# Two layers of cross-attention and quantised feed-forward: merged clips and exponentials, one moved rounding, a division in two parts, halved last products

## The chip, the cores and the metric

The kernel runs on one core of one Trainium2 chip. The metric is the device time of one execution in microseconds (us). The core has five engines that work beside each other: TensorE (PE: matmuls, and transposes as matmuls; PEld are its weight loads), VectorE (DVE), ScalarE (ACT), GpSimd (POOL) and SyncE (SP, which here only issues DMAs). Data lie in SBUF, in 128 partitions; matmuls write to PSUM, which is used in banks of 128 x 512 float32.

## What is computed

The input x has 8 batches of 112 tokens with 512 features, the context has 8 batches of 375 rows. Four residual steps follow each other:

```
x = x + L0_xattn(layernorm(x), ctx, mask0)   # one head, softmax over masked context rows
x = x + L0_ffn(layernorm(x), w1, w2, w3)     # silu(gate) * up, then down; each a "bit linear"
x = x + L1_xattn(layernorm(x), ctx, mask1, Wq, Wk, Wv, Wo, ...)   # 16 heads of 32
x = x + L1_ffn(layernorm(x), wq_gate, wq_up, wq_down, scales)     # integer weights - 128, scaled
```

A bit linear rounds its activations to whole numbers of -128..127 by the row's largest value and its weights to -1, 0, 1, and multiplies those. The steps that the change touches:

```
# L0_ffn:   h = silu(bitlinear(xn, w1)) * bitlinear(xn, w2);  x + bitlinear(h, w3)
# L1_xattn: scores = clip(q k^T / sqrt(32), -50, 50), masked ones -50
            probs = softmax(scores);  ctx = probs v;  out = layernorm(0.05-scaled ctx Wo + bo)
# L1_ffn:   y = silu(h Wg * sg) * (h Wu * su);  x + (y Wd) * sd
```

## The kernel before, in words

The 896 tokens (8 x 112) are kept as 7 tiles of 128 rows (`tokens`, `xs[i]`), the hidden size 1408 as 11 blocks of 128. PE's and SP's instructions stand in program order as written; for long stretches DVE, ACT and POOL do so too (`tc.manual_schedule`), elsewhere the framework orders these three when the program is built. A tile of a pool is handed out again only when the instructions that use it are done, so pools add waits of their own.

The keys and values of the second attention (L194 and L203, evicted by L197 and L205) don't depend on anything else. They are produced by a generator, and `fill(n)` puts n of its steps where PE would wait otherwise.

**First feed-forward (L533 to L700).** For each tile i, `gate_up0` multiplies the turned, rounded row (bf16) with ternary weights in three column blocks: four gate matmuls into one PSUM tile, four up matmuls into another (L541), SiLU on ACT (L545), the product on DVE (L546). `ranges0` finds the quantiser's factor `fwd` (L293 to L303, small DVE steps). `round0` (L565) rounds the 1408 columns: one ACT step that adds a large constant (L567), and two POOL steps that take it off again (L570); it also forms a small factor on DVE (L308). `turn_gate0(i + 1)` (L355) transposes the next tile's row on PE (L350) and copies it from PSUM on ACT (L352). `turn_down0` does the same for the rounded 1408 columns, and `down0` multiplies them (L581) and adds the result to the tokens (L583). The loop at L621 calls for each i: `gate_up0(i)`, `ranges0(i)`, filler, `turn_down0(i - 1)`, `round0(i)`, filler, `turn_gate0(i + 1)`, `down0(i - 1)`.

**Queries (L727).** Two groups of tiles (4 and 3), four column blocks each: PE forms a sum of products (L735, L737) and a small correction `less` (L741) in a tile of the pool `ps_s`; DVE takes it off (L745).

**Second attention (L848 to L1000).** Loops over 8 batches b and 3 chunks c of 125 context rows. `scores(b, c)` takes four tiles of one PSUM bank each from `ps_s` (four buffers), one for each r of the four 32-row groups; each holds four heads (dc = 0..3) of 112 tokens, 448 columns. For each r follow a clip on DVE (L907) and an exponential on ACT (L908) into SBUF tiles `sets[...][r]`. `add(b)` sums two chunks' exponentials on POOL (L894; on DVE for the last batch), so that the denominators take two matmuls and not three for each r. `sums` forms denominators (L923) and numerators (L928) in PSUM; ACT copies both (L934, L935). In step c = 1 of the next batch `divide` takes the reciprocal of 4 x 112 columns in one DVE instruction (L939) and multiplies (L941). In step c = 2, `project_product(b - 2)` multiplies tile b - 2 with Wo (L800): the tile's 128 tokens end inside batch b - 1, since 112 isn't 128. `project_begin` and `project_end` add bias, normalise and add to the tokens (L806 to L825; a reciprocal root on POOL, L105 to L109; POOL then forms a factor at L812, which DVE uses at L819). `write4` (L834) and `transpose4` (L841) normalise and turn tile b - 3 for the second feed-forward. In the meantime its integer weights are loaded in pieces of 640 columns and converted (L866, L877, L879). STEPS says in which steps a filler step of keys and values is put; batch 4 has two instead of three.

**Second feed-forward (L1021 to L1068).** `gate_up1` works on a group of tiles (512 or 384 tokens wide). For each hidden block hc it takes a PSUM tile for gate and one for up, again from `ps_s`; eight matmuls into each (L1031, float32r, high and low part), SiLU on ACT (L1036), product on DVE (L1037), a rounded copy on ACT (L1039), the remainder on DVE (L1040). The last tile's output of the attention (`project(NT - 1)`) is put between blocks 1 and 2. Then `down1` multiplies for each of the tiles: 22 matmuls of 512 columns into one PSUM tile (L1049), and `finish` scales it (L1017), adds the tokens (L1018) and stores 128 x 512 values (L1019). Group 1's tiles are turned (L841) between group 0's down products. At run time a branch chooses another form of this stage for large weights (`feed_forward1_wide`), which isn't taken here.

Of the kernel before, what the change touches and what calls it, by code (L numbers as in the profile page):

```python
# [64 lines left out]

SPLIT = 2.0 ** -12
LESS = 1.0 - 2.0 ** -13


@with_exitstack  # L70
def two_layers(ctx: ExitStack, tc: tile.TileContext, x, ctxT, ctxN, mask0, mask1, w1, w2, w3,
# [167 lines left out]
    with tc.tile_pool(name="w0", bufs=1, side="right") as w0p, \  # L239
# [290 lines left out]
        with tc.tile_pool(name="work1", bufs=2, side="right") as work1:  # L530
# [90 lines left out]
            for i in range(2, NT):  # L621
                gate_up0(i)
                if i == 2:
                    steps_of(2, 2)
                elif i == 3:
                    next(preparing[2])
                elif i == 4:
                    next(preparing[3])
                if i == 4:
                    ranges0(i, 1)  # L630
                    next(preparing[3])
                    ranges0(i, 1)
                else:
                    ranges0(i, 2)
                if i == 4:
                    moments2(0)
                    moments2(2)
                elif i == 5:
                    small.append(stat)
                    ve = stat.tile([P, GROUPS[0][1]], F32, name="ln2a_ve")  # L640
                    nc.vector.tensor_scalar_add(ve, mv2[:, :, 1], LN_EPS)
                    rstd2 = rsqrt(ve, "ln2a")
                    small.pop()

                    def normal2(h, i):
                        nc.vector.tensor_scalar(h, xs[i], mv2[:, i, 0:1], rstd2[:, i:i + 1],
                                                ALU.subtract, ALU.mult)
                elif i == NT - 1:
                    for k in range(2):
                        write2(k, normal2, k, work1)  # L650
                fill(2 if i < 4 else 1)
                turn_down0(i - 1)
                if i == 2:
                    steps_of(2, 1)
                round0(i)
                if i == 2:
                    next(preparing[2])
                elif i == 3:
                    next(preparing[3])
                fill(1)  # L660
                if i < NT - 1:
                    turn_gate0(i + 1)
                if i == 2:
                    down0(0)
                    next(preparing[2])
                    next(preparing[2])
                down0(i - 1)
                if i == 3:
# [96 lines left out]
    with tc.tile_pool(name="g1p", bufs=1, side="right") as g1p:  # L765
        h2T[1] = [g1p.tile([P, KC, 384], F32R, name=f"h2T1_{k}") for k in range(3)]
        write = normaliser(xs[4:6], "ln2b")
        for i in range(4, 6):
            write2(i, write, i - 4, tailp)
            transpose2(i, ps_s)()  # L770
        next(asking)
        write2(6, normaliser(xs[6:], "ln2c"), 0, tailp)
        transpose2(6, ps_s)()
        for g in range(2):
            for _ in asking:
                pass
            asking = queries(1)
# [70 lines left out]
    with tc.tile_pool(name="work2", bufs=1, side="right") as work2, \  # L848
# [21 lines left out]
        def convert_integers():  # L870
            for raw, which, half, c, n in loaded:
# [12 lines left out]

        sets = [[work2.tile([P, KC, T], F32, name=f"e{i}{r}") for r in range(NR)]
                for i in range(NCK)]

        def add(b):  # L890
            add = (nc.gpsimd if b in ADD_POOL else nc.vector).tensor_add
            for r in range(NR):
                e, e1 = (sets[(b + c) % NCK][r][:CK] for c in range(2))
                add(e, e, e1)  # L894

        def scores(b, c):
            kT = kvs_of[b][0]
            ss = [ps_s.tile([CK, KC, T], F32, name="s") for r in range(NR)]
            for dc in range(KC):
                for r in range(NR):  # L900
                    rows = slice(r * HD, (r + 1) * HD)
                    nc.tensor.matmul(ss[r][:, dc, :], lhsT=kT[rows, dc, c * CK:(c + 1) * CK],  # L902
                                     rhs=qT[rows, dc, b * T:(b + 1) * T], start=True, stop=True)
            es = sets[(b + c) % NCK]
            for r in range(NR):
                e = es[r][:CK]
                nc.vector.tensor_scalar(e, ss[r], upper[:, c, b:b + 1], -CLIP, ALU.min, ALU.max)  # L907
                nc.scalar.activation(e, e, AF.Exp, scale=SC1)  # L908
            return es

# [25 lines left out]
                rdens[b] = rden  # L936

        def divide(b):
            nc.vector.reciprocal(rdens[b], rdens[b])  # L939
            cols = slice(b * T, (b + 1) * T)  # L940
            nc.vector.tensor_mul(qT[:, :, cols], qT[:, :, cols], rdens[b])  # L941


        STEPS = [3, 3, 3, 3, 2, 3, 3, 3]
# [5 lines left out]
        for b in range(B):  # L950
            for c in range(NCK):
# [18 lines left out]
                if c == 0:  # L970
                    while later:
                        later.pop()()
                    if b >= 3:
                        project_end(b - 3)
                elif c == 1 and b >= 1:
                    divide(b - 1)
                elif c == 2:
                    turned = 3 <= b < 3 + GROUPS[0][1]
                    if turned:
                        write4(b - 3)  # L980
                    if b >= 2:
                        project_product(b - 2)
                    if b == B - 1:

                        hits = ps_s.tile([1, 29], F32, name="s")
# [18 lines left out]
    with tc.tile_pool(name="work3", bufs=2, side="right") as work3, \  # L1004
# [10 lines left out]
        def finish(i, ps):  # L1015
# [2 lines left out]
            nc.vector.tensor_add(y, y, xs[i])  # L1018
            nc.sync.dma_start(out=rows_out[i * P:(i + 1) * P], in_=y)  # L1019

        def gate_up1(g, begin, end, gus):  # L1021

            n = (GROUPS[g][1] - GROUPS[g][0]) * P
# [17 lines left out]
                                     gus[0][:, hc, :n].bitcast(F32))  # L1041

        def down1(g, i, gus):
            ps = ps_d.tile([P, D], F32, name="down")
            j = i - GROUPS[g][0]
            for hc in range(HC):
                w, c = half_of(2, hc * D)
                for k in range(2):
                    nc.tensor.matmul(ps, lhsT=gus[k][:, hc, j * P:(j + 1) * P],  # L1049
                                     rhs=w[:, c:c + D], start=(hc == 0 and k == 0),  # L1050
                                     stop=(hc == HC - 1 and k == 1))
            finish(i, ps)

        def feed_forward1():
            gus = [work3.tile([P, HC, 512], F32R, name=f"gu_{k}", bufs=1) for k in range(2)]
# [3 lines left out]
            for i in range(*GROUPS[0]):  # L1059
# [1 line left out]
                    write4(GROUPS[1][0] + i)  # L1061
                down1(0, i, gus)
                if GROUPS[1][0] + i < NT:
                    transpose4(GROUPS[1][0] + i, ps_s, "s")()
# [5 lines left out]
        def feed_forward1_wide(g):  # L1070
# [27 lines left out]
            for i in range(i0, i1):  # L1098
# [5 lines left out]
                                     start=(hc == 0), stop=(hc == HC - 1))  # L1104
                finish(i, ps)

        is_wide = nc.values_load(wide[0:1, 0:1], min_val=0, max_val=P)
        with tc.If(is_wide == 0) as fits:
            feed_forward1()
        with fits.Else():  # L1110
            project(NT - 1)
            feed_forward1_wide(0)
            for i in range(*GROUPS[1]):
                write4(i)
                transpose4(i, ps_s, "s")()
            feed_forward1_wide(1)


def _laid_out(inputs):
# [63 lines left out]
```

## Time and profile before

| | |
|---|---|
| three runs | 517.44, 517.8, 518.0 us; median 517.8 |
| the profiled execution | 517.36 us, of which the span of instructions is 515.6 |
| granted TensorE clock, mean | 0.996 of full speed |
| DVE, clips L907 | 96 of 125 x 448, mean 676 ns |
| ACT, exponentials L908 | 96 of 125 x 448, mean 570 ns |
| POOL, sums L894 | 28, mean 1233 ns |
| DVE, reciprocals L939 | 8 of 128 x 448, mean 2942 ns |
| PE, last products L1049 | 154 of 128 x 512, mean 396 ns; 22 of them for each tile |
| output DMA | 7 of 256 KB, 2.0 us from issue to landing (median) |

A row of a group gives line, engine, operation, `out<-in` with shapes, and how often; then the busy time in us and the mean of one in ns. A row of the timeline gives the start in us, the duration of a group of like instructions in us, engine, line, names, shapes and count, and in brackets how long the engine had been idle before it and what ended that. Matmuls are pipelined: the end of a record is modelled and several records overlap, so the time that one costs is the step from start to start. A row of the waits gives the total in us, how often, and the longest.

### The profile page before, as it was taken

The numbers are of one execution on the slowest core, as the hardware profiler recorded it, in microseconds if no ns is written. First come the engines' busy times: TensorE is split into PE (matmuls) and PEld (weight loads), VectorE is DVE, ScalarE is ACT, GpSimd is POOL, SyncE is SP. The second block draws the span as 40 slices with busy tenths as digits, with TensorE's granted clock in tenths as the row PEclk, the third lists the DMA queues.
The fourth block names the chain that finished last, engine by engine and source line by source line (L and its number), as shares of the span: only waits on it lengthen the run. The fifth ranks groups of instructions, "written<-read, shape, count | busy, mean of one in ns | idle before, by whom it ended". The sixth has DMA issues, their size and how long they took to land.

```text
span 515.6 us, 8804 instructions
## 1 busy us (share of the span) xinstructions
PE 502.3 (97%) x3380; PEld 315.0 (61%) x3380; DVE 334.3 (65%) x801; ACT 252.4 (49%) x438; POOL 133.9 (26%) x221
## 2 busy tenths in 40 slices
PE   9999999999999999999999999999999999999995
PEld 6445554455545455686565465555555788889983
DVE  3642548767798986964676588997897753334432
ACT  0326656857565665336675375465665233103310
POOL 0000121110011164211551475574753430000000
PEclk9999999999999999999999999999999999999998
DMA  8997795200120100122421112012320000010001
GB/s 242 363 407 298 274 326 201 79 18 0 61 82 1 60 2 0 37 109 58 162 70 53 61 52 62 3 53 62 98 76 5 21 1 1 20 42 20 1 20 46
DMA packets 13343, 45.75 MB, mean 89 GB/s; under 512 B 2081, under 2 KB 3120, under 8 KB 12144
## 3 DMA queue, kind: packets, MB, share of 16 engines
q1 hardware_dynamic: 11744, 41.43, 23.4%
q0 software_dynamic: 1248, 3.70, 2.2%
q8 instruction: 28, 0.46, 0.4%
q14 instruction: 19, 0.16, 0.1%
q10 hardware_dynamic: 304, 0.01, 0.0%
HBM read 41.46 MB, written 1.84 MB: 84 GB/s over the span
## 4 chain that ended last, share of the span: by engine, by line
PE 47%; DVE 6%; POOL 2%; DMA 1%; ACT 1%; issue 1%; DVEq 0%; POOLq 0%
PE s L1031 14%; PE mm L203 8%; PE down L1049 7%; PE mm L800 4%; PE s L902 3%; PE num L928 2%; PE mm L194 2%; DVE e L907 2%; PE den L923 2%; DMA raw<-in_wd_dram 1%; PE mm L737 1%; PE mm L735 1%; PE s L741 1%; DVE e L939 1%; POOL ln_t L108 1%
## 5 line engine op out<-in xcount | busy, mean ns | idle before, releaser
L194 PE MATMUL mm<-cT,wk 128*128 128x375 f32 x256 | 87.6, 487 | 0.0
L203 PE MATMUL mm<-wv,cT 128*125 128x512 f32 x192 | 87.6, 599 | 0.0
L1031 PE MATMUL s<-h4T,w 128*128 128x512 f32 (+1 forms) x352 | 72.6, 367 | 0.2 <-PE num L928 0.2
L1031 PEld LDWEIGHTS s<-h4T,w 128*128 128x128 f32 x352 | 63.5, 188 | 8.8 <-PE num L928 0.5
L907 DVE TENSOR_SCALAR e<-s,upper 125x448 f32<-125x448 f32 x96 | 59.0, 676 | 14.7 <-PE s L902 13.9
L908 ACT ACTIVATE e<-e 125x448 f32<-125x448 f32 x96 | 51.7, 570 | 27.6 <-DVE e L907 27.0
L194 PEld LDWEIGHTS mm<-cT,wk 128*128 128x128 f32 x256 | 47.0, 191 | 27.6 <-issue 0.8
L203 PEld LDWEIGHTS mm<-wv,cT 128*125 128x125 f32 x192 | 34.5, 187 | 38.0 <-issue 36.4
L894 POOL TENSOR_TENSOR e<-e,e 125x448 f32<-125x448 f32 x28 | 33.7, 1233 | 14.9 <-PE num L928 14.9
L1049 PE MATMUL down<-w,gu 128*128 128x512 f32 x154 | 37.0, 396 | 0.0
L541 PE MATMUL mm<-w_q,q_qT 128*128 128x512 fp8e4 (+1 forms) x168 | 34.6, 361 | 1.5 <-ACT q_qT L352 1.1
L439 POOL DMA_DIRECT2D tokens<-x x14 | 10.7, 768 | 90.6 <-DVE x L433 64.0
L1049 PEld LDWEIGHTS down<-w,gu 128*128 128x128 f32 x154 | 28.6, 188 | 6.7
L1039 ACT CAST gu<-gu 128x512 fp32r<-128x512 f32 (+1 forms) x22 | 12.5, 567 | 39.6 <-DVE gu L1037 39.6
L877 ACT ACTIVATE w<-raw,zero_point 128x640 fp32r<-128x640 int32 (+2 forms) x29 | 22.6, 781 | 18.9 <-DMA raw<-in_wd_dram 7.6
L570 POOL TENSOR_SCALAR q<-gu 128x704 bf16<-128x704 f32 x14 | 10.8, 787 | 80.0 <-ACT gu L567 80.0
L902 PE MATMUL s<-qT,kv 32*125 32x112 f32 x768 | 29.3, 280 | 0.6 <-DVE qT L745 0.3
L1037 DVE SCALAR_TENSOR_TENSOR gu<-s,su,gu 128x512 f32<-128x512 f32 (+1 forms) x22 | 15.0, 684 | 21.9 <-PE s L1031 20.6
L902 PEld LDWEIGHTS s<-qT,kv 32*125 32x125 f32 x768 | 24.5, 183 | 7.1 <-issue 5.6
L541 PEld LDWEIGHTS <-q_qT 128*128 128x128 bf16 x168 | 16.4, 98 | 20.3 <-issue 1.8
L879 POOL TENSOR_SCALAR w<-raw 128x640 fp32r<-128x640 int32 (+2 forms) x29 | 19.8, 693 | 34.2 <-ACT w L877 33.9
L800 PE MATMUL mm<-wo,qT 128*128 128x512 f32 x56 | 25.8, 603 | 1.0 <-DVE qT L941 1.0
(236 smaller groups left out, 787.5 us busy)
## 6 DMA issues: line engine op xcount, KB each, us to landing
cT<-in_ctxT_dram SPq DMA_DIRECT2D x13, 750.0 KB, 6.1
raw<-in_w_dram SPq DMA_DIRECT2D x6, 1408.0 KB, 19.2
cN<-in_ctxN_dram SPq DMA_DIRECT2D x8, 768.0 KB, 4.4
raw<-in_wg_dram SPq DMA_DIRECT2D x8, 320.0 KB, 3.1
raw<-in_wu_dram SPq DMA_DIRECT2D x8, 320.0 KB, 3.0
raw<-in_wd_dram SPq DMA_DIRECT2D x8, 320.0 KB, 3.1
out_dram<-d SPq DMA_DIRECT2D x7, 256.0 KB, 2.0
wk<-in_wk_dram SPq DMA_DIRECT2D x4, 256.0 KB, 4.8
```

The costliest lines, as they stand in the source:

```text
L194: nc.tensor.matmul(ps[dc], lhsT=wk_s[:, kc, dc * P:(dc + 1) * P], rhs=cT[:, kc, :], start=(kc == 0), stop=(kc == KC - 1))
L203: nc.tensor.matmul(ps, lhsT=cT[:, kc, c * CK:(c + 1) * CK], rhs=wv_s[:, kc, :], start=(kc == 0), stop=(kc == KC - 1))
L541: nc.tensor.matmul(ps[:, :n], lhsT=qT[:, kc, :], rhs=w[:, kc * H + n0:kc * H + n0 + n], start=(kc == 0), stop=(kc == KC - 1))
L800: nc.tensor.matmul(ps, lhsT=qT[:, kc, i * P:(i + 1) * P], rhs=wo_s[:, kc, :], start=(kc == 0), stop=(kc == KC - 1))
L877: nc.scalar.activation(t, raw, AF.Square, bias=zero_point, accum_out=squares[:, k:k + 1])
L879: nc.gpsimd.tensor_scalar(t, raw, -128.0, 1.0, ALU.add, ALU.mult)
L894: add(e, e, e1)
L902: nc.tensor.matmul(ss[r][:, dc, :], lhsT=kT[rows, dc, c * CK:(c + 1) * CK], rhs=qT[rows, dc, b * T:(b + 1) * T], start=True, stop=True)
L907: nc.vector.tensor_scalar(e, ss[r], upper[:, c, b:b + 1], -CLIP, ALU.min, ALU.max)
L908: nc.scalar.activation(e, e, AF.Exp, scale=SC1)
L1031: nc.tensor.matmul(ps[:, :n], lhsT=w[:, c:c + P], rhs=h4T[k][:, kc, :n], start=(kc == 0 and k == 0), stop=(kc == KC - 1 and k == 1))
L1049: nc.tensor.matmul(ps, lhsT=gus[k][:, hc, j * P:(j + 1) * P], rhs=w[:, c:c + D], start=(hc == 0 and k == 0), stop=(hc == HC - 1 and k == 1))
```

## The change

Five edits:

1. The pool `ps_s` (four tiles of one bank) becomes a pool of two tiles of two banks. `scores` takes two of these pairs and puts r = 0, 1 into the first and r = 2, 3 into the second. Clips, exponentials and POOL's sums handle a pair (2 x 448 columns) in one instruction. All else that took tiles from `ps_s` (the queries' correction, the turned tiles, gate and up of the second feed-forward) gets halves of a pair, by the new class `Halves`; a pair is free again when both halves' users are done.
2. For i = 4 in the first feed-forward, `round0(4)` is called after `turn_gate0(5)` and not ahead of it.
3. `divide` works in two parts: the tokens that complete a tile of 128 first (reciprocal and product), then the rest. The first part has 16, 32, 48, 64, 80 or 96 tokens for b = 1 to 6; b = 0 and b = 7 have a single part.
4. The last tile's down products are formed in two halves of 256 columns (44 matmuls instead of 22), each with a scaling, an addition and a DMA of its own (`finish_last`).
5. `hits`, one small product at the end of the attention, gets a pair of its own.

```diff
+class Halves:
+    def __init__(self, pool):
+        self.pool, self.left = pool, []
+
+    def tile(self, shape, dtype, name):
+        if not self.left:
+            pair = self.pool.tile([P, 2, 512], F32, name="s")
+            self.left = [pair[:, 0, :], pair[:, 1, :]]
+        n = 1
+        for d in shape[1:]:
+            n *= d
+        t = self.left.pop(0)[:shape[0], :n]
+        return t if len(shape) == 2 else t.rearrange("p (a b) -> p a b", a=shape[1])
...
-                round0(i)
+                if i != 4:
+                    round0(i)
...
                 if i < NT - 1:
                     turn_gate0(i + 1)
+                if i == 4:
+                    round0(i)
...
-    ps_s = ctx.enter_context(tc.tile_pool(name="ps_s1", bufs=4, space=PSUM))
+    ps_pair = ctx.enter_context(tc.tile_pool(name="ps_s1", bufs=2, space=PSUM))
+    ps_s, ps_turned = Halves(ps_pair), Halves(ps_pair)
...
-            for r in range(NR):
-                e, e1 = (sets[(b + c) % NCK][r][:CK] for c in range(2))
+            for h in range(NR // 2):
+                e, e1 = (twos[(b + c) % NCK][h][:CK] for c in range(2))
                 add(e, e, e1)
...
-            ss = [ps_s.tile([CK, KC, T], F32, name="s") for r in range(NR)]
+            ss = [ps_pair.tile([P, 2, 512], F32, name="s") for h in range(NR // 2)]
...
-            for r in range(NR):
-                e = es[r][:CK]
-                nc.vector.tensor_scalar(e, ss[r], upper[:, c, b:b + 1], -CLIP, ALU.min, ALU.max)
+            for h in range(NR // 2):
+                e = twos[(b + c) % NCK][h][:CK].rearrange("p a k t -> p a (k t)")
+                nc.vector.tensor_scalar(e, ss[h][:CK, :, :KC * T], upper[:, c, b:b + 1], -CLIP,
+                                        ALU.min, ALU.max)
                 nc.scalar.activation(e, e, AF.Exp, scale=SC1)
...
         def divide(b):
-            nc.vector.reciprocal(rdens[b], rdens[b])
-            cols = slice(b * T, (b + 1) * T)
-            nc.vector.tensor_mul(qT[:, :, cols], qT[:, :, cols], rdens[b])
+            n = (b + 1) * T - (b + 1) * T // P * P
+            for t0, t1 in ((0, T - n), (T - n, T)):
+                rden, of = rdens[b][:, :, t0:t1], qT[:, :, b * T + t0:b * T + t1]
+                if t1 > t0:
+                    nc.vector.reciprocal(rden, rden)
+                    nc.vector.tensor_mul(of, of, rden)
...
+        def finish_last(i, ps, half):
+            cols = slice(half * D // 2, (half + 1) * D // 2)
+            y = tailp.tile([P, D], F32, name="d", bufs=2)[:, :D // 2]
+            nc.vector.tensor_mul(y, ps, sd_s[:, cols])
+            nc.vector.tensor_add(y, y, xs[i][:, cols])
+            nc.sync.dma_start(out=rows_out[i * P:(i + 1) * P, cols], in_=y)
...
-            for hc in range(HC):
-                w, c = half_of(2, hc * D)
-                for k in range(2):
-                    nc.tensor.matmul(ps, lhsT=gus[k][:, hc, j * P:(j + 1) * P],
-                                     rhs=w[:, c:c + D], start=(hc == 0 and k == 0),
-                                     stop=(hc == HC - 1 and k == 1))
-            finish(i, ps)
+            halves_of = (0, 1) if i == NT - 1 else (None,)
+            for half in halves_of:
+                n, n0 = (D, 0) if half is None else (D // 2, half * D // 2)
+                ps = ps_d.tile([P, D], F32, name="down")[:, :n]
+                for hc in range(HC):
+                    w, c = half_of(2, hc * D)
+                    for k in range(2):
+                        nc.tensor.matmul(ps, lhsT=gus[k][:, hc, j * P:(j + 1) * P],
+                                         rhs=w[:, c + n0:c + n0 + n],
+                                         start=(hc == 0 and k == 0),
+                                         stop=(hc == HC - 1 and k == 1))
+                if half is None:
+                    finish(i, ps)
+                else:
+                    finish_last(i, ps, half)
```

More of the change, by code (lines that the diff above doesn't have):

```diff
@@ L769, in two_layers @@
             write2(i, write, i - 4, tailp)
-            transpose2(i, ps_s)()
+            transpose2(i, ps_turned)()
         next(asking)
         write2(6, normaliser(xs[6:], "ln2c"), 0, tailp)
-        transpose2(6, ps_s)()
+        transpose2(6, ps_turned)()
         for g in range(2):
@@ L880, in convert_integers @@
             loaded.clear()
-        sets = [[work2.tile([P, KC, T], F32, name=f"e{i}{r}") for r in range(NR)]
+        twos = [[work2.tile([P, 2, KC, T], F32, name=f"e{i}{h}") for h in range(NR // 2)]
                 for i in range(NCK)]
+        sets = [[two[r // 2][:, r % 2] for r in range(NR)] for two in twos]
+        ps_turned.left.clear()
         def add(b):
             add = (nc.gpsimd if b in ADD_POOL else nc.vector).tensor_add
-            for r in range(NR):
-                e, e1 = (sets[(b + c) % NCK][r][:CK] for c in range(2))
+            for h in range(NR // 2):
+                e, e1 = (twos[(b + c) % NCK][h][:CK] for c in range(2))
                 add(e, e, e1)
@@ L901, in scores @@
                     rows = slice(r * HD, (r + 1) * HD)
-                    nc.tensor.matmul(ss[r][:, dc, :], lhsT=kT[rows, dc, c * CK:(c + 1) * CK],
+                    nc.tensor.matmul(ss[r // 2][:CK, r % 2, dc * T:(dc + 1) * T], lhsT=kT[rows, dc, c * CK:(c + 1) * CK],
                                      rhs=qT[rows, dc, b * T:(b + 1) * T], start=True, stop=True)
-            es = sets[(b + c) % NCK]
-            for r in range(NR):
-                e = es[r][:CK]
-                nc.vector.tensor_scalar(e, ss[r], upper[:, c, b:b + 1], -CLIP, ALU.min, ALU.max)
+            for h in range(NR // 2):
+                e = twos[(b + c) % NCK][h][:CK].rearrange("p a k t -> p a (k t)")
+                nc.vector.tensor_scalar(e, ss[h][:CK, :, :KC * T], upper[:, c, b:b + 1], -CLIP,
+                                        ALU.min, ALU.max)
                 nc.scalar.activation(e, e, AF.Exp, scale=SC1)
-            return es
+            return sets[(b + c) % NCK]
         def sums(b, c, es):
@@ L983, in two_layers @@
                     if b == B - 1:
-                        hits = ps_s.tile([1, 29], F32, name="s")
+                        hits = Halves(ps_pair).tile([1, 29], F32, name="s")
                         nc.tensor.matmul(hits, lhsT=ones[:, :1], rhs=over, start=True, stop=True)
@@ L1043, in down1 @@
         def down1(g, i, gus):
-            ps = ps_d.tile([P, D], F32, name="down")
             j = i - GROUPS[g][0]
-            for hc in range(HC):
-                w, c = half_of(2, hc * D)
-                for k in range(2):
-                    nc.tensor.matmul(ps, lhsT=gus[k][:, hc, j * P:(j + 1) * P],
-                                     rhs=w[:, c:c + D], start=(hc == 0 and k == 0),
-                                     stop=(hc == HC - 1 and k == 1))
-            finish(i, ps)
+            halves_of = (0, 1) if i == NT - 1 else (None,)
[13 more added lines that the diff above has]
+                    finish_last(i, ps, half)
         def feed_forward1():
@@ L1063, in feed_forward1 @@
                 if GROUPS[1][0] + i < NT:
-                    transpose4(GROUPS[1][0] + i, ps_s, "s")()
+                    transpose4(GROUPS[1][0] + i, ps_turned, "s")()
             gus = [work3.tile([P, HC, 512], F32R, name=f"gu_{k}", bufs=1) for k in range(2)]
@@ L1105, in feed_forward1_wide @@
                 finish(i, ps)
+        for halved in ps_s, ps_turned:
+            halved.left.clear()
         is_wide = nc.values_load(wide[0:1, 0:1], min_val=0, max_val=P)
@@ L1109, in two_layers @@
             feed_forward1()
+            for halved in ps_s, ps_turned:
+                halved.left.clear()
         with fits.Else():
@@ L1114, in two_layers @@
                 write4(i)
-                transpose4(i, ps_s, "s")()
+                transpose4(i, ps_turned, "s")()
             feed_forward1_wide(1)
+            for halved in ps_s, ps_turned:
+                halved.left.clear()
 def _laid_out(inputs):
```

## The prediction

> **What bounds the kernel now.** I read the page's busy shares, slices and chain first, to see whether there is anything but TensorE to shorten.
>
> ```profile
> PE 502.3 (97%) x3380; PEld 315.0 (61%) x3380; DVE 334.3 (65%) x801; ACT 252.4 (49%) x438; POOL 133.9 (26%) x221
> ...
> PE   9999999999999999999999999999999999999995
> ...
> PE 47%; DVE 6%; POOL 2%; DMA 1%; ACT 1%; issue 1%; DVEq 0%; POOLq 0%
> ```
>
> PE is full in every slice but the last. No matmul work goes away in this change, so only PE's stalls and the tail can be won. PE's waits name three of them, without those that are shorter than the stretch by which a matmul's record outlasts the next start:
>
> ```profile
> PE mm L541 <- ACT q_qT L352: 1.1, 1, 1.1
> PE mm L800 <- DVE qT L941: 1.0, 1, 1.0
> ...
> PE mm L841 <- ACT kv L197: 0.5, 1, 0.5
> ```
>
> By starts of matmuls (what exceeds the usual step) these cost 1.29, 1.24 and 0.70 us; three scores products (L902) lose 0.59 at 268.8, 0.57 at 302.3 and about 0.2 at 362.3 to clips on DVE (L907). Then I read the timeline at each of these places, at the one where the change puts a new wait, and at the end.
>
> **Turned copy ahead of the rounding: -0.8.**
>
> ```profile
> 177.13 0.16 DVE L303 SCALAR_TENSOR_TENSOR q_fwd<-q_fwd,q_y 128x1 f32<-128x1 f32 x1
> ...
> 177.39 1.56 ACT L567 ACTIVATE gu<-gu,rounder,q_fwd 128x1408 f32<-128x1408 f32 x1 [2.34 <-DVE q_fwd L303]
> ...
> 178.82 0.66 DVE L205 COPY kv<-mm 125x512 f32<-125x512 f32 x1
> 178.86 0.56 ACT L352 COPY q_qT<-s 128x512 bf16<-128x512 bf16 x1
> ...
> 179.47 3.79 PE L541 MATMUL mm<-w_q,q_qT 128*128 128x512 fp8e4 x17 [1.12 <-ACT q_qT L352]
> ```
>
> The copy stands behind a rounding that waits for q_fwd, while ACT idles 2.34 us. Its transposes ended near 176.0, so ahead of it the copy (0.56) fits into that idle time, and the rounding still starts at 177.39. It is followed by its two POOL roundings (0.79 each) as before; SP isn't passed. PE could go on at 178.2. Next late: the up product needs the PSUM tile that the first L205 frees at 179.5; four gate matmuls (0.86) from 178.2 end before, so up starts about 179.55 instead of 180.33. Gain 0.8; 0.4 if L205 slips, 1.29 if nothing is late.
>
> **Clip and exponential of two groups: -1.0.** Four clips take 2.46 with a last record of 0.676, so one every (2.46-0.68)/3 = 0.595. DVE's slope is (750-618)/128 = 1.03 ns per column (L1037 at 512 and 384), 448 columns are 0.46, the fixed part 0.13; a clip of 896 is then 0.93+0.13 = 1.06, a call 2.12 instead of 2.38: -0.25. ACT the same way: four in 1.96, slope (687-581)/128 = 0.83, so -0.2 a call. POOL's sums keep 4.8 us for a pair of sets. Times 24 that is 6 us of DVE, hidden under PE except where a stall is: at 268.8 two shortened calls precede, the third group's matmul starts 0.5 earlier, -0.46; at 302.3 one call, -0.2; at 362.3 -0.1; at 371.6 L197 comes behind the exponentials, -0.2. Sum -1.0, between 0 (they meet another wait) and -2.
>
> **Division in two parts: -0.8.**
>
> ```profile
> 322.14 2.94 DVE L939 RECIPROCAL e<-e 128x448 f32<-128x448 f32 x1
> 325.18 0.63 DVE L941 TENSOR_TENSOR qT<-qT,e 128x448 f32<-128x448 f32 x1
> 325.92 2.46 DVE L907 TENSOR_SCALAR e<-s,upper 125x448 f32<-125x448 f32 x4
> 328.29 0.53 DVE L834 TENSOR_SCALAR d<-tokens,mv,rstd 128x512 f32<-128x512 f32 x1
> ```
>
> Batch 3's first part is 48 of 112 tokens: reciprocal 2.94x48/112 = 1.26, product 0.3 to 0.55, from 321.9 (clips 0.25 shorter) to about 323.7. PE is free for L800 at 324.63: the 1.24 go. The second part costs some 0.3 us of DVE more (fixed parts), so the clips and write L834 end at about 328.65 where PE, now done at 328.16, wants to transpose: 0.45 come back. Net -0.8 (-0.4 to -1.24). The other batches' +0.3 lies under filler products of 3.7 us.
>
> **A wait that is added: +1.3.** The second feed-forward takes its gate and up tiles from the same two pairs. Before, gate of block h waited for ACT's read of gate h-2; now the whole pair must be free, so it waits for DVE's product with up of h-2 (L1037), read half a block (1.87 us) later. Mostly that has 2 to 3 us to spare. One place hasn't:
>
> ```profile
> 412.19 0.75 DVE L1037 SCALAR_TENSOR_TENSOR gu<-s,su,gu 128x512 f32<-128x512 f32 x1
> ...
> 414.86 0.26 POOL L812 TENSOR_SCALAR ln_f<-ln_f,rs 128x1 f32<-128x1 f32 x1
> 415.15 0.75 DVE L819 SCALAR_TENSOR_TENSOR tokens<-d,ln_f,tokens 128x512 f32<-128x512 f32 x1 [2.21 <-POOL ln_f L812]
> ```
>
> In the changed program as built, DVE has L819, which waits for POOL until 415.12, ahead of block 2's product. That product then runs at about 415.82 to 416.57; behind it queue the remainder's subtraction and block 3's product, for which gate 5 waits about 1 us less than it takes to get there. Gate 4 would start at 415.24 and must wait to 416.6: +1.3 (0 if DVE's order proves harmless, 1.6 with slow handovers).
>
> **Last down products in halves: -0.85.**
>
> ```profile
> 504.67 4.60 PE L1049 MATMUL down<-w,gu 128*128 128x512 f32 x19
> ...
> 505.62 5.47 SPq L1019 DMA_DIRECT2D out_dram<-d  x2
> 509.31 0.69 DVE L1017 TENSOR_TENSOR d<-down,sd 128x512 f32<-128x512 f32 x1 [3.72 <-PE down L1049]
> 510.03 0.69 DVE L1018 TENSOR_TENSOR d<-d,tokens 128x512 f32<-128x512 f32 x1
> ```
>
> Both DVE steps at 256 columns: 0.69-256x1.03 ns = 0.43, twice 0.26 saved: -0.53. The output DMA carries 128 KB instead of 256 (landing 2.0 us; loads of 320 KB take 3.1): -0.3, between 0 and -0.6. The first half's steps and DMA lie under the second half's 2.5 us of products; SP issues one DMA more, ahead of the last, with nothing else queued. What matters is PE: 44 matmuls of 256 columns for 22 of 512. The step at 512 is (4.60-0.40)/18 = 0.2335; at 384 (48 of them in 8.48, last 0.336) 0.1733; the line through both gives 0.113 at 256, its slope alone (0.47 ns a column) 0.120, and I take 0.117: 44x0.117 = 5.15 against 22x0.2335 = 5.14, nothing.
>
> Against halving speaks the Trainium skill, "TensorE: Matmul & The Clock Gate", section "LDWEIGHTS (loading the stationary operand)": a load takes about P/1.2 ns, whatever the width that streams after it, 107 ns for 128 columns. If 22 more loads were in the open, that would be an estimated +2.35 by that page, and +22x0.188 = 4.1 by the load records of L1049 (188 ns). The trace has a 188 ns record on every load of the 384-wide products too, and yet they follow each other in 0.1733, all of it streaming by that slope: the loads are hidden, and a record isn't a step. At 256 columns the cover is only 0.113 to 0.120, hardly above the page's 107 ns, so it is near its edge: if a load sets the step, 0.139 (the load record of L841's transposes, also 128x128) gives +1.0, 0.188 gives 44x0.188-5.14 = +3.1. Below nothing: 44x0.113 is -0.15. I keep 0.117, the 384-wide row being the nearest.
>
> **Sum** against the profiled execution (517.36, its span of 515.6 and 1.8 around it): -0.8-1.0-0.8+1.3-0.85 = -2.15, 515.2. That execution lies 0.44 below the median of 517.8, so against the median it is 515.65; I say 515.6.
>
> **Rivals.**
> The gate never waits (DVE reaches block 2's product in time): the 1.3 falls away, 514.3. For it: DVE is mostly idle there. Against: the order is fixed and L819's wait for POOL stands in the trace. 0.2.
> The stalls move on: clip, division and copy run into the next late thing nearly completely, leaving -1.0 of their 2.6; with the gate's wait and the tail 517.2, no change. For it: each stall has another instruction within 0.5 to 0.8 us. Against: the next ones were looked up one by one. 0.15.
> The halves' added loads are in the open: at one place, the last 44 matmuls, 22 loads of 0.188 come on top, +4.1: 519.8, slower. It decides from 2.15/22 = 0.098 a load on (0.145 for a loss beyond 0.2%). For it: the thinner cover; against it: 0.1733 at 384 with loads of 0.188. 0.08.
> The change doesn't do what it says: the copy's place, the pairs, the parts and the halves are all in the built program, so not counted.
> My own case has 0.57.
>
> **How the numbers follow.** A measurement can tell about 0.2%, 1.04 us, from no change: faster is below 516.8, slower above 518.8. My case's own range is 514.4 to 516.7 by the bounds of its terms, which hardly all go one way. For 8 in 10 the range goes from 514.0 (first rival) to 517.9 (second). Faster: nearly all of my case and of the first, 0.75; same: the second and a load half in the open, 0.15; slower: the third, and a gate wait that repeats over several blocks, 0.10.
>
> **What would show it.** PE starts L541 (tile 5) without a wait on L352, and up starts about 0.8 earlier; clips of 896 follow each other at 1.06, exponentials at 0.84; L800 near 324 has no wait on DVE, the transposes behind it wait for L834; gate 4 waits for DVE with L819 ahead; half matmuls step at 0.11 to 0.12; the last two DVE steps take 0.43. I am wrong if gates wait block after block, if half matmuls step at 0.14 or more, or if clips of 896 take twice those of 448.

## The result: slower, and the profile after

The changed kernel takes 521.28 us (median of five runs, 520.47 to 523.1), the kernel before 517.8 in the same comparison: ratio 1.0072, 95% interval 1.0055 to 1.009. The forecast of 515.6 with a range of 514.0 to 517.9 was wrong, in sign as well. The profiled execution takes 520.83 with a span of 518.9, so the span grew by 3.3 us.

PE is as busy as before (502.4 us), so the 3.3 us are waits. PE's waits of the changed kernel, the longest of them (line, what it waited for, total us, times, longest):

```profile
PE s L244 <- DVE h2T L250: 2.3, 2, 1.5
PE mm L862 <- ACT kv L214: 1.6, 1, 1.6
PE mm L862 <- DVE d L855: 1.4, 1, 1.4
PE s L1066 <- DVE gu L1072: 1.2, 1, 1.2
...
PE mm L821 <- DVE qT L969: 0.5, 1, 0.5
```

The lines are the changed kernel's: L244, L821, L862, L930, L932, L968, L969, L918, L855 and L1072 are L227, L800, L841, L907, L908, L939, L941, L894, L834 and L1037 of before. The wait for the turned copy is gone, that for the division's product halved. Four others are new or longer. Two of them had been forecast: the gate's (L1066), and, at 0.45 us, that for the write (L855).

PE executes the same matmuls in the same order in both kernels (but for the last tile), so they can be set against each other one by one: how much later each starts in the changed kernel, and where that difference jumps. This tells what each place is worth, with what is given back later counted in:

| place (time in the kernel before) | forecast, us | measured, us |
|---|---|---|
| 179.5 turned copy ahead of the rounding | -0.8 | -0.7 (-1.3, +0.5 at the up product, +0.1 later) |
| 220.6 transposes of tile 5 | none | +1.7 |
| 268.8, 302.3, 362.3 scores behind clips | -0.5, -0.2, -0.1 | -0.3, -0.2, -0.2 |
| 310.5 transposes, batch 3 | none | +0.2 |
| 325.9 projection, batch 4 | -1.24 | -0.5 |
| 329.4 transposes, batch 4 | +0.45 | +1.6 |
| 371.6 transposes, batch 6 | -0.2 | +1.1 |
| 415.2 gate 4 | +1.3 | +1.4 |
| last tile and end | -0.85 | -0.8 |
| sum | -2.1 | +3.3 |

Three places make 4.9 of the 5.4 us between forecast and measurement: 220.6 (1.7), the pair at 325.9 and 329.4 (1.9), and 371.6 (1.3).

**220.6.** The timeline of the changed kernel, PE, ACT and DVE (start, duration, instruction, idle time before):

```profile
219.48 0.60 PE L244 MATMUL s<-ident,d 128*128 128x128 f32 x4
220.11 0.60 ACT L247 ACTIVATE h2T<-s 128x512 fp32r<-128x512 f32 x1 [0.66 <-PE s L244]
220.81 0.68 DVE L250 TENSOR_TENSOR h2T<-s,h2T 128x512 fp32r<-128x512 f32 x1
...
221.55 0.66 PE L244 MATMUL s<-ident,d 128*128 128x128 f32 x4 [1.47 <-DVE h2T L250]
```

Tiles 4 and 5 are turned into the two halves of one pair. Before, all eight transposes ran in a row:

```profile
220.18 1.03 PE L227 MATMUL s<-ident,d 128*128 128x128 f32 x8
```

Now tile 5's start 0.06 after DVE has done with tile 4's half, although that is another bank: a pair counts as one tile, and a write into it stands behind every earlier reading of it.

**325.9 to 331.2.** The same view at batch 4, with POOL:

```profile
322.34 1.34 DVE L968 RECIPROCAL e<-e 128x192 f32<-128x192 f32 x1
323.73 4.23 POOL L918 TENSOR_TENSOR e<-e,e 125x896 f32<-125x896 f32 x2 [0.91 <-PE num L952]
323.79 2.24 DVE L969 TENSOR_TENSOR qT<-qT,e 128x192 f32<-128x192 f32 x1
...
326.08 3.70 PE L821 MATMUL mm<-wo,qT 128*128 128x512 f32 x8 [0.53 <-DVE qT L969]
...
330.48 0.54 DVE L855 TENSOR_SCALAR d<-tokens,mv,rstd 128x512 f32<-128x512 f32 x1
```

The first part's reciprocal ends at 323.68, as forecast (about 323.15 on a kernel that was 0.6 ahead there). Its product, 192 columns, takes 2.24 us: it starts 0.06 after the first of POOL's two sums (2.08 of the 4.23) has started, and ends 0.21 after that sum has ended at 325.82. Clips and write follow late, and the transposes (L862) wait for the write until 331.16.

**371.6.** In batch 6 the two products take 2.00 and 1.20 us, the clips and exponentials behind them are late, and so is the eviction L214 behind those, for which PE waits:

```profile
366.31 2.00 DVE L969 TENSOR_TENSOR qT<-qT,e 128x320 f32<-128x320 f32 x1
...
369.21 1.20 DVE L969 TENSOR_TENSOR qT<-qT,e 128x128 f32<-128x128 f32 x1
...
373.62 0.56 ACT L214 ACTIVATE kv<-mm,bk 128x375 f32<-128x375 f32 x1
...
374.23 0.66 PE L862 MATMUL mm<-ident,d 128*128 128x128 f32 x4 [1.64 <-ACT kv L214]
```

### The profile page after: what moved, and what is told of

Its sections match the earlier page's. It is cut to its first block, busy times and chain, and to the rows that moved or that the text cites. A ratio compares the mean times of both kernels' runs of the same rounds, so it can differ in the third digit from the quotient of the medians.

```text
span 518.9 us, 8697 instructions
## 1 busy us (share of the span) xinstructions
PE 502.4 (97%) x3402; PEld 315.0 (61%) x3402; DVE 334.9 (65%) x765; ACT 246.8 (48%) x390; POOL 130.8 (25%) x207
## 4 chain that ended last, share of the span: by engine, by line
PE 46%; DVE 9%; POOL 2%; issue 1%; DMA 1%; ACT 1%; DVEq 0%; POOLq 0%; SPq 0%
PE s L1066 11%; PE mm L220 8%; PE down L1088 7%; PE mm L211 4%; PE s L926 4%; PE num L952 3%; PE mm L821 3%; DVE e L968 2%; DVE e L930 2%; PE den L947 2%; DVE qT L969 1%; PE mm L758 1%; PE mm L756 1%; PE s L762 1%; POOL ln_t L125 1%
## 5 line engine op out<-in xcount | busy, mean ns | idle before, releaser
L1066 PE MATMUL s<-h4T,w 128*128 128x512 f32 (+1 forms) x352 | 72.8, 367 | 1.4 <-DVE gu L1072 1.2
L1066 PEld LDWEIGHTS s<-h4T,w 128*128 128x128 f32 x352 | 63.5, 188 | 10.3 <-DVE gu L1072 1.7
L930 DVE TENSOR_SCALAR e<-s,upper 125x896 f32<-125x896 f32 x48 | 53.0, 1146 | 16.4 <-PE s L926 14.5
L932 ACT ACTIVATE e<-e 125x896 f32<-125x896 f32 x48 | 44.8, 946 | 35.9 <-DVE e L930 34.0
L1088 PE MATMUL down<-w,gu 128*128 128x512 f32 (+1 forms) x176 | 37.0, 367 | 0.0
L918 POOL TENSOR_TENSOR e<-e,e 125x896 f32<-125x896 f32 x14 | 30.5, 2201 | 15.1 <-PE num L952 13.3
L1088 PEld LDWEIGHTS down<-w,gu 128*128 128x128 f32 x176 | 29.8, 188 | 5.7
L1071 ACT ACTIVATE gu<-s,sg 128x512 f32<-128x512 f32 (+1 forms) x22 | 14.0, 636 | 35.8 <-PE s L1066 31.2
L1072 DVE SCALAR_TENSOR_TENSOR gu<-s,su,gu 128x512 f32<-128x512 f32 (+1 forms) x22 | 15.0, 683 | 24.0 <-ACT gu L1071 22.8
L952 PEld LDWEIGHTS num<-e,kv 125*32 125x32 f32 x768 | 18.4, 110 | 13.6 <-issue 7.9
```

The lines of the kernel that those rows point to most:

```text
L930: nc.vector.tensor_scalar(e, ss[h][:CK, :, :KC * T], upper[:, c, b:b + 1], -CLIP, ALU.min, ALU.max)
L952: nc.tensor.matmul(num[r * HD:(r + 1) * HD, dc, :], lhsT=v[:, c, head], rhs=es[r][:CK, dc, :], start=(c == 0 and dc == 0), stop=(c == NCK ...
L1066: nc.tensor.matmul(ps[:, :n], lhsT=w[:, c:c + P], rhs=h4T[k][:, kc, :n], start=(kc == 0 and k == 0), stop=(kc == KC - 1 and k == 1))
```

## Theory and rival

Theory: DVE's product of the division has both its inputs in SBUF, and it can't run while a POOL sum, which reads SBUF too, is in flight. It waits out the whole instruction. So longer sums mean longer waits, and two products meet two of them. The Trainium skill, "SBUF — State Buffer", section "Who interferes with whom", says this: a VectorE instruction with two SBUF inputs contends with a GpSimd instruction that reads SBUF, and the one that comes second blocks until the first is done. The lines above fit that (the product ends 0.21 after the sum); the runs below test it. Rival: DVE is late because of the fixed costs of the second part, or because merged clips and exponentials hold something up, whatever POOL does. Beside this stand the waits for whole pairs.

## Experiments

Ratios are to the kernel before, with 95% intervals. "Own pools" is an edit that most have in common: pairs for the scores alone, and four single-bank tiles each for the queries and the second feed-forward.

A run's time is the span of its instructions and something outside it. Outside lie 1.8 to 1.9 us by the medians in most of these kernels, but 2.35 in e1 and 2.1 to 2.2 in e6, e7 and e11. I don't know why; differences of 0.3 to 0.5 us between those and the others are therefore not read as waits.

**e1, own pools.**

```diff
-    ps_pair = ctx.enter_context(tc.tile_pool(name="ps_s1", bufs=2, space=PSUM))
-    ps_s, ps_turned = Halves(ps_pair), Halves(ps_pair)
     ps_mm = ctx.enter_context(tc.tile_pool(name="ps_mm1", bufs=2, space=PSUM))
+    ps_s = singles.enter_context(tc.tile_pool(name="ps_s1", bufs=4, space=PSUM))
+    ps_turned = ps_s
...
+            tc.tile_pool(name="ps_pair", bufs=2, space=PSUM) as ps_pair, \   # attention
...
+            tc.tile_pool(name="ps_s2", bufs=4, space=PSUM) as ps_s, \        # second feed-forward
```

> The changed kernel with the pairs in the attention's scores alone: the queries and the second feed-forward take single-bank tiles from pools of their own again (four tiles each). My theory, from the drift of PE between the two traces, is that two places wait for a pair as a whole: the transposes of tile 5 ahead of the queries' third block (1.6 us) and gate 4 of the second feed-forward (1.3 us). Both should go: 521.3 - 3.0 = 518.3. Rival: the losses come from the attention alone (longer instructions, the division), and PE meets other waits at the two places, so no more than 0.5 us comes back: 520.8 or more.

519.52 us, 1.0038 (1.0024 to 1.0051). Both waits are gone: PE's difference to before doesn't jump at 220.6 nor at 415.2. But only 1.8 us of 3.0 came back, mainly because the edit brought a wait of its own: PE's later start jumps by 1.4 at the first query product. The product tiles lie in other banks than before, and in e4, which shares the edit, that product starts 0.1 after the last DVE addition of the first feed-forward (L600) has ended. e5 below removes the wait by putting these tiles into other banks.

**e2, sums of 448 columns again.** `for r in range(NR)` over `sets[...][r]` in `add`.

> The changed kernel with POOL's sums of exponentials per 448 columns again (28 instructions of 1.1 us instead of 14 of 2.1). Theory: DVE's product of the division has two inputs in SBUF and doesn't run until the POOL sum in flight is done, so its wait is as long as one POOL instruction: the worst product falls from 2.24 to at most 1.3 us, and the two stalls ahead of the transposes in batches 4 and 6 shrink by about 0.9 each: 521.3 - 1.8 = 519.5. Rival: it is the second part of the division and its fixed costs that make DVE late, whatever POOL does: 521.3, products of 2 us stay.

519.0 us, 1.0029 (1.0017 to 1.004), 2.3 less than the changed kernel. The longest product beside sums of exponentials takes 1.22 us. In batch 4 the changes are -1.05 and +1.35 instead of -0.5 and +1.6, in batch 6 +0.1 instead of +1.1. The rival falls: clips, exponentials and the two parts are those of the changed kernel.

**e3, division in one part**, sums of 896.

> The changed kernel with the division in one part. Theory (a product waits for the POOL sum in flight): one product per batch meets one wait of up to 2.1 us instead of two, the clips behind it come 1.3 to 2 us earlier in batches 4 and 6, and PE starts about 0.3 later on the projection in batch 4: 521.3 - 2.1 = 519.2. Rival (the division in two parts is a gain of its own and the merged clips lose): 521.3 + 0.8 = 522.1.

518.12 us, 1.0012 (1.0005 to 1.0019): 3.2 less, more than I expected, and the opposite of what my prediction's account gives. In batch 4 there is no wait at the transposes, and in batch 6 nothing is left of the +1.1. What is left above the kernel before are the two waits for pairs. So merged sums by themselves cost next to nothing; with merged sums the two parts cost 3.2 us (e3), and with the two parts the merging costs 2.3 (e2).

**e4, own pools and sums of 448.**

> Both: pairs in the scores alone, and POOL's sums per 448 columns; clips and exponentials merged, division in two parts, copy moved, halves as in the changed kernel. Theory: 521.3 - 3.0 - 1.8 = 516.5, below the kernel before (517.8). Rival (a third cause in the merged clips or exponentials): 517.8 or more.

516.88 us, 0.9981 (0.9974 to 0.9988). No third cause shows: past the first 8 us, the lasting losses of PE against the kernel before are the 1.4 at the first query product and the 1.35 in batch 4. The division in two parts still brings nothing here: at batch 4 its timeline shows

```profile
322.87 4.71 POOL L920 TENSOR_TENSOR e<-e,e 125x448 f32<-125x448 f32 x4 [0.66 <-PE num L954]
323.17 1.04 DVE L971 TENSOR_TENSOR qT<-qT,e 128x192 f32<-128x192 f32 x1
...
329.49 0.63 PE L864 MATMUL mm<-ident,d 128*128 128x128 f32 x4 [1.15 <-DVE d L857]
```

The product of 192 columns waits for one sum of 1.13 and takes 1.04; the projection starts at once, and the transposes start 1.3 late (they wait 1.15).

**e5, e6, e8: lengths of the sums, with and without the parts.** Own pools with the product tiles at the other end of PSUM (`side="right"`), e5 with sums of 448 in one part, e6 with sums of 224 (`[:CK, k:k + 2]`) in two parts, e8 with sums of 224 in one part.

> As the version with pairs in the scores alone and sums of 448, but the queries' product tiles lie in other PSUM banks (so that the first of them doesn't wait for the last addition of the first feed-forward, 1.4 us in that version), and the division is in one part again. Theory: the 1.4 go; in batch 4 PE waits about 1.0 for the product as before the change but no longer 1.3 for the transposes: 516.9 - 1.4 - 0.3 = 515.2. Rival, by my prediction's account (the division in parts is worth 0.8): 516.9 - 1.4 + 0.8 = 516.3.

515.5 us, 0.9969 (0.9961 to 0.9977). The rival, my own account of the parts, would have had 516.3.

> The same pools, the division in two parts, and POOL's sums per 224 columns (56 instructions of some 0.65 us). Theory: a product waits for one POOL instruction, now 0.65 at most, so both parts together lose at most 0.7 instead of 1.2 and the transposes in batch 4 wait about 0.7 instead of 1.3: 516.9 - 1.4 - 0.6 = 514.9. Rival (the waits don't depend on the length of a sum): 515.5 and a transposes' wait of 1.3.

515.48 us (five runs, 514.26 to 515.9), 0.9962 (0.9949 to 0.9975). The wait at the transposes is 0.3 us, and the two products take 0.36 and 0.42. That is less than the theory asked for, and luck: each product happened to start 0.05 to 0.06 before the sum in flight ended (in e9 the same product takes 0.82). The median is 0.6 above what I expected and the same as e5's; the 0.3 to 0.4 more outside the span are part of that.

> The same pools, sums per 224 columns, the division in one part. Theory: the single product waits at most 0.65, in batch 4 perhaps not shorter than the 0.63 of before; PE's stall there stays at about 1.0 (the reciprocal of 2.94 sets it), the transposes don't wait: 515.1. Rival: the 28 added POOL instructions make the sums late for the denominators: over 516.

515.02 us, 0.9962 (0.9951 to 0.9973), as expected.

**e7, the kernel before with the division in two parts.**

> The kernel before with the division in two parts and nothing else. By my prediction's account -0.8: 516.9. Theory now (each product waits for a POOL sum of 1.1): the projection in batch 4 starts 1.1 earlier, the transposes behind it wait about 1.4 for the writes: 517.6 + 0.3 = 517.9.

518.16 us, 1.0011 (1.0001 to 1.0022): about +0.6, not -0.8. In its trace the product of 192 happened to run ahead of a sum (0.36), so batch 4 won 0.5 and batch 6 0.4; a product of 1.44 in batch 3's step and a wait of 0.6 at 310.5 behind it took most of that back. These places alone give a gain of 0.3 in its trace (an execution that was late by 2.6 in its first 8 us already). Some 0.3 of the loss lie outside the span; the rest isn't settled.

**e9, two parts for batch 3 alone** (`if b == 3 else T`), sums of 224.

> As the version with pools of their own (product tiles in other banks) and sums per 224 columns, with the division in two parts for batch 3 alone, the only one that PE waits for. Theory: batch 4's stall of 1.1 goes but for some 0.3 at the transposes, and the other batches' products keep one wait each: 0.7 to 0.8 less than undivided (515.0), 514.3. Rival (the parts are worth nothing by themselves): 515.0.

515.13 us, 0.9958 (0.9942 to 0.9973): the gain over e8 that I expected isn't there. The product of 192 met a sum again (0.82), and the transposes waited 0.9 where the projection won 1.05. The same product took 0.36 in e6: neither edit fixes where it falls beside the sums.

**e10, the kernel before with the halves alone.**

> The kernel before with the last tile's down products in halves and nothing else. By my prediction, and by the end of the changed kernel's trace (half products every 0.117, DVE steps of 0.43): -0.7 to -0.85, 516.7. Rival (the added weight loads or the shorter DMA rows cost it): 517.4 or more.

516.77 us, 0.9983 (0.9973 to 0.9994): -0.7 by the medians, -0.9 by the ratio, as forecast.

**e11 and e12, sums after the products.** The direct test: nothing is shortened, only the overlap is taken away.

```diff
                 if c == 2 and b in ADD_POOL:
+                    if b > 0:
+                        nc.gpsimd.tensor_scalar(after_product, qT[:, 0, b * T - 1:b * T], 1.0, 1.0,
+                                                ALU.mult, ALU.mult)
                     add(b)
```

> The changed kernel with pairs in the scores alone (product tiles in other banks), the sums of 896 and the division in two parts kept, but with one small POOL instruction (128 x 1) ahead of each batch's sums that reads what the division's last product wrote: POOL's sums then begin after both products and not beside them. It adds nothing that the output needs. Theory (a product waits only while a POOL sum is in flight): products of 192 and 256 columns take 0.36 and 0.43 as in the runs where no sum lay beside them, PE has no wait ahead of the projection in batch 4 and about 0.3 to 0.5 at the transposes, as my prediction's sum had it: 519.5 - 1.4 - 1.8 - 0.8 = 515.5. Rival (the long sums or the parts themselves cost the time, or the later sums hold up the denominators): 518 or more.

514.79 us, 0.9947 (0.9931 to 0.9963), 0.7 below what I expected. The timeline of e11 at batch 4:

```profile
320.51 1.34 DVE L970 RECIPROCAL e<-e 128x192 f32<-128x192 f32 x1
...
321.96 0.36 DVE L971 TENSOR_TENSOR qT<-qT,e 128x192 f32<-128x192 f32 x1
...
323.85 3.70 PE L823 MATMUL mm<-wo,qT 128*128 128x512 f32 x8
324.01 0.42 DVE L971 TENSOR_TENSOR qT<-qT,e 128x256 f32<-128x256 f32 x1
324.60 0.19 POOL L985 TENSOR_SCALAR after_product<-qT 128x1 f32<-128x1 f32 x1 [3.61 <-DVE qT L971]
324.75 4.40 POOL L920 TENSOR_TENSOR e<-e,e 125x896 f32<-125x896 f32 x2
...
327.38 0.60 PE L864 MATMUL mm<-ident,d 128*128 128x128 f32 x4
```

The same sums of 896 and the same two parts as in the changed kernel, but the product takes 0.36 instead of 2.24, PE waits neither at the projection nor at the transposes. No run has exactly these pools with sums of 896 beside the products; the nearest is e1, which has other banks as well and the wait of 1.4 that comes with them. So what shows the cause is this place, and not the total alone.

The later sums do hold up something, in other steps: the write L857 (L834 of before), which takes 0.54 with no sum beside it.

```profile
304.93 4.14 POOL L920 TENSOR_TENSOR e<-e,e 125x896 f32<-125x896 f32 x2
...
306.93 2.43 DVE L857 TENSOR_SCALAR d<-tokens,mv,rstd 128x512 f32<-128x512 f32 x1
...
309.51 0.63 PE L864 MATMUL mm<-ident,d 128*128 128x128 f32 x4 [0.21 <-DVE d L857]
```

It started 0.06 before the second sum, took 2.43, and ended 0.29 after that sum; twice more in e11 it took 2.43 as well. Here the transposes start 0.4 later for it (310.5 in the kernel before).

> The same with sums of 448. Theory: once no sum lies beside the products their length is of no account, so the time is that of the run before within 0.3 us: 515.5 (sums of four make POOL 0.4 us later). Rival: shorter sums are better by themselves: 1 us less.

513.76 us, 0.9929 (0.9914 to 0.9945), the fastest of all: 3.4 us below the kernel before in the same comparison, 517.12. I expected e11's time within 0.3, and by the medians the rival came out, 1.0 less (with overlapping intervals of the ratios). Up to PE's last matmul the traces don't show it (506.5 and 506.7). Of the 1.0, about 0.4 lie outside the span (2.15 against 1.78 by the medians). In e11's profiled execution 5.3 us pass from the last DVE instruction to the end of the span, in e12's 4.8. Why, stays open.

The runs side by side at batch 4 (change of PE's start against the kernel before; products of batch 3):

| kernel | sums | division | products, us | projection | transposes |
|---|---|---|---|---|---|
| changed | 896 | two parts | 2.24, 0.52 | -0.5 | +1.6 |
| e4 | 448 | two parts | 1.04, 0.67 | -1.05 | +1.35 |
| e6 | 224 | two parts | 0.36, 0.42 | -1.05 | +0.3 |
| e11 | 896, later | two parts | 0.36, 0.42 | -1.05 | 0 |
| e12 | 448, later | two parts | 0.36, 0.42 | -1.05 | +0.45 |
| e3 | 896 | one part | 0.70 | -0.2 | 0 |
| e5 | 448 | one part | 0.82 | -0.1 | 0 |

## Why the prediction was wrong, point by point

**Turned copy, -0.8: right** (-0.7). PE went on at 178.15 and the up product was next late, as said.

**Clip and exponential, -1.0: right in mechanism, sizes near.** A clip of 896 has a mean of 1.146 with steps of 1.06, an exponential 0.946 with steps of some 0.83 to 0.85; the three places of scores gave the -0.8 put on them. (With no sum beside the product, in e11 and e12, 268.8 alone gave -0.8.) The -0.2 at 371.6 was covered over by the late products; in e5 and e8, with the division in one part, it is -0.4.

**Division, -0.8: the step that failed.** "Reciprocal 2.94x48/112 = 1.26, product 0.3 to 0.55". The reciprocal was right (1.34), the product was not: 2.24 in batch 4. The two instructions were costed alone, though POOL's sums lay beside them in the trace. Worse, the change made those sums twice as long, and I put POOL's merging at nothing because the total of 4.8 us stayed (it fell to 4.4). What a neighbour waits for is the length of one instruction, not the total. The division was worth -0.8 by the sum; measured were +1.1 in batch 4 and +1.1 in batch 6. With the overlap removed (e11, e12), batch 4 gave -1.05 and -0.6: the arithmetic held once its silent condition did, though e11 lost 0.4 again at 310.5 to the write that its later sums hold. "The other batches' +0.3 lies under filler products" failed with it.

The page of before had the warning. Two group rows of DVE, both tensor_tensor with two SBUF inputs (busy us, mean ns, idle before):

```profile
L941 DVE TENSOR_TENSOR qT<-qT,e 128x448 f32<-128x448 f32 x8 | 8.3, 1038 | 0.8
...
L1018 DVE TENSOR_TENSOR d<-d,tokens 128x512 f32<-128x512 f32 x7 | 4.8, 690 | 0.2
```

Fewer columns, and half as long again. That is the wait for POOL, already in the kernel before. I used the one instance of 0.63 and didn't ask why the mean was 1.04. That instance was short because it began at 325.18, when the sum in flight had 0.08 left. Making the reciprocal shorter moved the product to the start of a sum, where there was a whole one to wait out.

**The wait that is added: right where I looked, and one was missed.** Gate 4 waits as forecast. In the timeline of the changed kernel:

```profile
417.77 0.75 DVE L840 SCALAR_TENSOR_TENSOR tokens<-d,ln_f,tokens 128x512 f32<-128x512 f32 x1 [2.91 <-POOL ln_f L833]
418.44 0.74 DVE L1072 SCALAR_TENSOR_TENSOR gu<-s,su,gu 128x512 f32<-128x512 f32 x1
419.24 0.97 PE L1066 MATMUL s<-h4T,w 128*128 128x512 f32 x3 [1.24 <-DVE gu L1072]
```

Block 2's product stands behind L840, which waits for POOL, and gate 4 starts behind that product. With own pools the wait is gone (e1, e4). But I asked only when a pair can be handed out again, not what happens between its two halves: at 220.6 the second half's first write waits for the first half's reader, 1.7 us. The sum had no term for it.

**Last down products, -0.85: right** (-0.8; e10 alone -0.7 by the medians and -0.9 by the ratio). Half products of the changed kernel, and DVE's last two steps:

```profile
508.78 4.59 PE L1088 MATMUL down<-w,gu 128*128 128x256 f32 x38
...
513.41 0.42 DVE L1052 TENSOR_TENSOR d<-down,sd 128x256 f32<-128x256 f32 x1 [1.68 <-PE down L1088]
513.87 0.42 DVE L1053 TENSOR_TENSOR d<-d,tokens 128x256 f32<-128x256 f32 x1
```

(4.59-0.28)/37 = 0.1165 a product, 0.117 forecast; loads recorded at 188 ns stay hidden under it. The rival of loads in the open is refuted.

The rivals as a whole: none of the three was what happened, and with every term at its worst bound the sum gives only +0.3 (518.1). The loss lay in what the sum had no term for: the POOL sum beside the product, and the write into a pair's second half. Slower had a chance of 0.10. The one on the slower side sat in the wrong place, and the second, stalls that move on, had too small a price: it took what is next late to be 0.5 to 0.8 away, and the product itself became 1.9 us longer.

## What to carry to other kernels

An instruction's cost in a sum holds only beside the neighbours it had in the trace: where two engines can block each other, cost the pair, and take a mean well above that of a like instruction elsewhere as the sign. Merging instructions on one engine lengthens the longest wait of whoever shares something with it, even if the totals fall, so a merge and a split that meet at the same place have to be looked at together. Moving the long instruction away from one neighbour puts it beside another, as e11's write shows. When two buffers become one tile, follow each write between its halves too, not only the tile's return to the pool.

## What the runs showed of the hardware that I had not expected

DVE's product with two SBUF inputs ends only after the POOL sum in flight: 192 columns took 0.36 with no sum beside it (e11), 1.04 beside sums of 1.13 (e4) and 2.24 beside sums of 2.08 (the changed kernel). It goes the other way too: a POOL sum of 448 that met a product took up to 1.57 instead of 1.13 (before). DVE's reciprocal with one SBUF input isn't held: 2.94 for 448 columns with and without sums beside it.

Two whole tensors aren't needed for it. The write reads one tensor and two columns of scalars (`d<-tokens,mv,rstd`), and it took 0.54 alone, 1.24 beside a sum of 1.13 (e4) and 2.43 beside sums of 2.1 (e11). What sets it apart from the reciprocal isn't tested here.

Ordering POOL's sums behind the products, so that the two no longer overlap, took e12 below e4 by 3.1 us by the medians and 2.7 by the ratios, of which the wait at the first query product is 1.4.
